# First attention: the first batch's first steps are held in front of the weights' on each engine, and the first weights load in three parts

## The chip, the cores and the metric

The kernel runs on one core of a Trainium2 chip. A core has five engines that run side by side, each through its own list of instructions in a fixed order: TensorE (PE, matrix products; PEld is its loading of weights), VectorE (DVE), ScalarE (ACT), GpSimd (POOL) and SyncE (SP, which here issues most of the transfers). An instruction waits until the results it reads are there, and everything behind it in its engine's list waits with it. The metric is the device time in microseconds (us) of one execution, lower is better; the median of several runs is what is compared.

## The reference, cut to what matters

Four layers work in turn on x of shape (4, 512, 128): each is a cross attention on a context of 32 rows and a feed-forward part. Only the beginning of the first layer is touched:

```python
x = x + L0_xattn(layernorm(x), ctx)       # the first attention
x = x + L0_ffn(layernorm(x))              # 8 experts, each token goes to one
...

def L0_xattn(tgt, memory, ...):
    qkv = tgt @ qkv_w.T + qkv_b
    q, k, v = jnp.split(qkv, 3, axis=-1)
    ...                                    # scores masked to their diagonal: attn is the identity
    sa = einsum('bnm,bmc->bnc', attn, v) @ sa_out_w.T + sa_out_b
    x = _ln(tgt + sa, ln1_g, ln1_b)
    ...                                    # cross attention of 8 heads with the context
    x = _ln(x + ca, ln2_g, ln2_b)
    ff = relu(x @ lin1_w.T + lin1_b) @ lin2_w.T + lin2_b
    return _ln(x + ff, ln3_g, ln3_b)
```

Because the self attention sees its diagonal alone, it is one product of the normalised x with a matrix that is made from `qkv_w` and `sa_out_w`.

## The kernel before

**Tiling.** A batch is 512 tokens, held as 4 tiles of 128 tokens by 128 columns. Everything is float32. A step of a batch is mostly one instruction over 128x512, or four over 128x128. A float32 product appears in the profile as two matmuls where it isn't a transposition, so "four products" is `x8`.

**Who sets the order.** The program is written as Python generators. `together` takes one step of each generator in turn, so the written order is a mixture of the chains; its argument `late` says in which round each chain enters. Out of that a scheduler makes the list of each engine when the program is built: it takes what it believes to be ready, by the written order where several are. So a change at one place can reorder the lists a long way on. `tc.issue_after(instruction)` puts all that is written inside its scope behind that instruction, on that instruction's engine. The object `queued` holds such scopes open until the tables of activation functions are next exchanged, in the second layer.

**The loads.** They are issued in the written order: batch 0's x (256 KB) on SP and the constants (`cst`) on ACT; then on SP the columns and rows of biases, the first weights `w0` (896 KB: sa_v, sa_o, ca_q, ca_k, ca_v, ca_o of 128 columns each, lin1 and lin2 of 512), x1; on ACT `adds`; then on SP x2, x3, `w1`, the first experts' weights and the masks. An issue on SP waits until an earlier transfer that used the same of eight semaphores has landed.

**The chains of the first attention.** `l0_weights` makes the folded weights: a matrix for the self attention (L477 to L484: `folded`, two products, a copy to `w_sa`), then kT of the context (`scaled_keys`, L295 and L297), the keys per batch (`folded_keys`: POOL L266, PE L319, ACT L321), the values (L338, L343), and a folded bias of lin1 (L506, L507). `attend0(g)` does one batch:

- a normalisation of x (`normed`): DVE statistics L203, L204, L206; ACT L208, L209; DVE L213 to L216, the shift c by L225 and L227; ACT L230 writes `xn`. POOL L516 adds a bias to x in place.
- `transposed`: PE L244, ACT L246; the self attention's product PE L256 and the sum y on DVE L468
- a second normalisation (DVE L232 writes z) and its transposition
- the cross attention in two halves (`attend`): PE L396, DVE L381 and L382, ACT L383, PE L409, ACT L411, PE L415, DVE L424 and L425; then the output product (L244, L246, L256) and a second y (L468)
- a normalisation with ACT's L230, the feed-forward part (PE L538, ACT L539, PE L544, a third y at L468), a last normalisation, and POOL's L558 and L559, which add the result to x (DVE for batch 3)

`noted(g)` follows in the same chain: it normalises the new x (L203 again, L234), writes it to memory, transposes it and makes the routing logits (PE L578, DVE L586). After all four batches the routing is completed, and POOL gathers tokens by it (L811).

The stage is started by these lines:

```python
    together(
        [
            l0_weights(w0),
            *(queue(attend0(g), noted(g)) for g in range(B)),
            early(),
            queue(ready("few1", l1_weights()), ready("slots", l1_ffn_weights()), ready("few2", l2_weights())),
        ],
        late={0: 0, 1: 0, 2: 3, 3: 6, 4: 9, 5: 14, 6: 14},
    )
```

Of the kernel before, what the change touches and what calls it, by code (L numbers as in the profile page):

```python
# [13 lines left out]
ALU = mybir.AluOpType  # L14
AX = mybir.AxisListType

P = 128
D = 128
B = 4
# [15 lines left out]
_W0 = [("sa_v", 128), ("sa_o", 128), ("ca_q", 128), ("ca_k", 128), ("ca_v", 128), ("ca_o", 128),  # L35
       ("lin1", 512), ("lin2", 512)]
# [18 lines left out]
def _offsets(spec):  # L55
    at, n = {}, 0
    for name, cols in spec:
        at[name] = (n, n + cols)
        n += cols
    return at, n  # L60
# [11 lines left out]
def tile_kernel(ctx: ExitStack, tc: tile.TileContext, I, out):  # L72
    nc = tc.nc
    const = ctx.enter_context(tc.tile_pool(name="const", bufs=1))
# [11 lines left out]
    l0 = l0_scope.enter_context(tc.tile_pool(name="l0", bufs=1))  # L86

    def psum(name="pt", fill=0):


        pt = ps.tile([P, 512], F32, tag="ps", name=name)
        for _ in range(fill):
            nc.tensor.matmul(pt[:, :P], lhsT=ident, rhs=ident, start=True, stop=True)  # L93
        return pt

    def small(cols, name="small", dtype=F32):
        return sm.tile([P, cols], dtype, tag=f"{name}{cols}", name=name)
# [2 lines left out]


    wide = {}

    def packed(key, spec, rows=P, pool=const, queue=nc.sync):
        at, n = _offsets(spec)
        t = pool.tile([rows, n], F32, tag=key, name=key)
        queue.dma_start(t, I[key])
        for name in ("switch", "router", "w_g"):
            if name in at:
                wide[name] = t[:, at[name][0] : at[name][0] + P]  # L110
        return {name: t[:, a:b] for name, (a, b) in at.items()}
# [9 lines left out]
    def together(chains, skew=0, late=()):  # L121


        waiting = [(late[i] if i in late else i * skew, c) for i, c in enumerate(chains)]
        running = []
        now = 0
        while waiting or running:
            running += [c for at, c in waiting if at == now]
            waiting = [(at, c) for at, c in waiting if at > now]
            for c in list(running):  # L130
                try:
                    next(c)
                except StopIteration:
                    running.remove(c)
            now += 1

    def queue(*steps):

        for c in steps:
            yield from c  # L140

    def batch(g):
        xg = const.tile([P, NJ, D], F32, tag=f"x{g}", name=f"x{g}")
        nc.sync.dma_start(xg, I["x"][g].rearrange("(j p) d -> p j d", p=P))
        return xg

    X = [batch(0)]
    C = packed("cst", _CST, queue=nc.scalar)
    col = packed("cols", _COLS)
    row = packed("rows", _ROWS, rows=1)  # L150
    W = packed("w0", _W0, pool=l0)
    X.append(batch(1))
    adds = const.tile([P, len(_ADDS), D], F32, tag="adds", name="adds")
    nc.scalar.dma_start(adds, I["adds"].partition_broadcast(P))
    add = {name: adds[:, i, :] for i, name in enumerate(_ADDS)}
    X += [batch(2), batch(3)]
    W.update(packed("w1", _W1))
    f0w1 = moe.tile([P, NEXP, 512], F32, tag="w1", name="f0w1")
    f0w2 = moe.tile([P, NEXP, 4, D], F32, tag="w2", name="f0w2")
# [11 lines left out]
    ident = C["ident"]  # L171
# [17 lines left out]
    queued = ctx.enter_context(ExitStack())  # L189
# [8 lines left out]
    def moments(src, p=P, n=NJ):  # L198

        st = sm.tile([P, n, 6], F32, tag=f"st{n}", name="st")  # L200
        mv = sm.tile([P, n, 2], F32, tag=f"mv{n}", name="mv")
        for j in range(n):
            nc.vector.bn_stats(st[:p, j, :], src[:, j, :])  # L203
            nc.vector.bn_aggr(mv[:p, j, :], st[:p, j, :])  # L204
        v = small(n, "v")[:p]
        nc.vector.tensor_scalar(v, mv[:p, :, 1], EPS, None, ALU.add)  # L206
        y = small(n, "y")[:p]
        nc.scalar.activation(y, v, AF.Ln)  # L208
        nc.scalar.activation(y, y, AF.Exp, scale=-0.5)  # L209
        yield  # L210

        t = small(n, "t")[:p]
        nc.vector.tensor_tensor(t, y, y, ALU.mult)  # L213
        nc.vector.scalar_tensor_tensor(t, t, -0.5, v, ALU.mult, ALU.mult)
        r = small(n, "r")[:p]
        nc.vector.scalar_tensor_tensor(r, t, 1.5, y, ALU.add, ALU.mult)  # L216
        return mv[:p], r

    def normed(src, tag, plus=0.0, act=False, p=P, n=NJ, bufs=B, pool=wk, into=None):

        mv, r = yield from moments(src, p, n)
        y = pool.tile([P, n, D], F32, tag=tag, name=tag, bufs=bufs) if into is None else into
        if plus or act:
            c = small(n, "c")[:p]
            nc.vector.scalar_tensor_tensor(c, mv[:, :, 0], -1.0, r, ALU.mult, ALU.mult)  # L225
            if plus:
                nc.vector.tensor_scalar(c, c, plus, None, ALU.add)  # L227
        for j in range(n):
            if act:
                nc.scalar.activation(y[:p, j, :], src[:, j, :], AF.Identity, bias=c[:, j : j + 1], scale=r[:, j : j + 1])  # L230
            elif plus:
                nc.vector.tensor_scalar(y[:p, j, :], src[:, j, :], r[:, j : j + 1], c[:, j : j + 1], ALU.mult, ALU.add)  # L232
            else:
                nc.vector.tensor_scalar(  # L234
                    y[:p, j, :], src[:, j, :], mv[:, j, 0:1], r[:, j : j + 1], ALU.subtract, ALU.mult
                )
        yield
        return y

    def transposed(src, tag="xnT", fill=0):  # L240

        pt = psum(fill=fill)
        for j in range(NJ):
            nc.tensor.transpose(pt[:, j * P : (j + 1) * P], src[:, j, :], ident)  # L244
        y = wk.tile([P, S], F32, tag=tag, name=tag, bufs=B)
        nc.scalar.copy(y, pt)  # L246
        yield
        return y

# [42 lines left out]
    def scaled_keys(w, bias, scale, rows=P):  # L292

        pt = psum()
        nc.tensor.matmul(pt[:rows, : B * M], lhsT=w, rhs=C["ctxT"], start=True, stop=True)  # L295
        kT = wk.tile([P, B * M], F32, tag="kTc", name="kTc")
        nc.vector.tensor_scalar(kT[:rows], pt[:rows, : B * M], 0.0 if bias is None else bias, scale, ALU.add, ALU.mult)  # L297
        return kT
# [175 lines left out]
    def l0_weights(w):  # L474


        fa = folded(W["sa_v"], bias=col["sa_bv"])  # L477
        ob = l0.tile([1, D], F32, tag="ob", name="ob")
        nc.vector.tensor_scalar(ob, row["sa_o_b"], 1.0 / D, None, ALU.mult)
        pt = psum()  # L480
        nc.tensor.matmul(pt[:, :D], lhsT=ones_row, rhs=ob, start=True, stop=False)
        nc.tensor.matmul(pt[:, :D], lhsT=fa, rhs=W["sa_o"], start=False, stop=True)
        w["sa"] = l0.tile([P, D], F32, tag="w_sa", name="w_sa")
        nc.scalar.copy(w["sa"], pt[:, :D])  # L484
        yield
        kT = scaled_keys(W["ca_k"], col["ca_bk"], 0.25)
        wq = folded(W["ca_q"], col["ca_bq"], add["ln1_g"], add["ln1_b"])
        with_value_bias("ca_o_b", col["ca_bv"], W["ca_o"])
        yield
        w["keys"] = padded(l0, "keys0", 8 * M)  # L490
        for b in range(B):
            folded_keys(w["keys"], wq, kT, 8, C["hm8"], bs=(b,))
            if b % 2:
                yield
        w["vals"] = head_values("v0", context_rep, W["ca_v"], 8, M, C["vm8"], C["hi32"], l0)


        w["rest"] = rest = l0.tile([P, 2, D], F32, tag="rest", name="rest")
        nc.gpsimd.tensor_tensor(rest[:, 0], add["ln1_b"], add["ln1_g"], ALU.subtract)
        nc.gpsimd.tensor_tensor(rest[:, 0], rest[:, 0], add["ca_o_b"], ALU.add)  # L500
        nc.gpsimd.tensor_tensor(rest[:, 1], add["ln2_b"], add["lin2_b"], ALU.add)
        yield
        w["lin1_b"] = lin1_b = l0.tile([P, 4], F32, tag="lin1b", name="lin1_b")
        pt = psum()
        for f in range(4):
            nc.tensor.matmul(pt[:, f : f + 1], lhsT=W["lin1"][:, f * P : (f + 1) * P], rhs=col["ln2_b"], start=True, stop=True)  # L506
        nc.vector.tensor_tensor(lin1_b, pt[:, :4], col["lin1_b"], ALU.add)  # L507
        nc.gpsimd.tensor_scalar(W["lin1"], W["lin1"], col["ln2_g"], None, ALU.mult)
        yield
# [833 lines left out]
    w0 = {}  # L1343
    attend0 = l0_xattn(w0)
# [17 lines left out]
    def noted(g):  # L1362
        yield from route0(g)
        routed0.append(g)

    def early():

        while len(routed0) < B - 1:
            yield
        yield from part0(0, (B - 1) * NJ)  # L1370

    together(
        [
            l0_weights(w0),
            *(queue(attend0(g), noted(g)) for g in range(B)),
            early(),
            queue(ready("few1", l1_weights()), ready("slots", l1_ffn_weights()), ready("few2", l2_weights())),
        ],
# [285 lines left out]
```

## Time and profile before

| | us |
|---|---|
| median of 3 runs | 649.58 |
| lowest and highest run | 647.67 and 649.80 |
| the profiled execution | 642.63 |
| its span | 640.8 |
| gather of routed tokens starts, in the span | 146.16 |
| TensorE busy | 530.2 |
| VectorE busy | 331.7 |
| ScalarE busy | 237.9 |
| GpSimd busy | 150.6 |

The profile is of one execution and can differ from the median. In a timeline a line is: start in us from the span's start, duration in us, engine, line of the program, operation, what it writes and reads with shapes, how many instructions are merged (`x4`), and in brackets how long the engine had been idle and what ended the wait. Instructions of one group can be interleaved with others, so groups overlap. A table of stretches gives, for each, the busy time of the engines named, with the number of instructions; then the clock granted to TensorE (1.00 is full), the share of the transfer engines and GB/s.

### The profile page before, as it was taken

To read this page: it belongs to the slowest core of one execution; us is meant where nothing else is said; L and a number is where in the kernel's file an instruction comes from. 1 tells how busy PE (TensorE), PEld (TensorE's weight loads), DVE (VectorE), ACT (ScalarE), POOL (GpSimd) and SP (SyncE) were. 2 spreads that over 40 slices of the span, in tenths; PEclk is the share of its full clock that TensorE was granted. 3 is DMA by queue.
4 is the path that set the end of the run, shared out by engine and by line. 5 is a ranking of instruction groups with operands and counts; after the bars stand their busy time and mean duration, and the time that the engine had idled before them with its cause. 6 is when DMAs were issued, how large, how long until landed. Compare 5 with 4: busy or idle time off the path is not lost.

```text
span 640.8 us, 9381 instructions
## 1 busy us (share of the span) xinstructions
PE 530.2 (83%) x3344; PEld 417.3 (65%) x3344; DVE 331.7 (52%) x1379; ACT 237.9 (37%) x538; POOL 150.6 (24%) x187
## 2 busy tenths in 40 slices
PE   2568889836998888899644999991899799999996
PEld 2557667626986664799431788881478676767764
DVE  4686654583397542688762222214777763323232
ACT  2353555411245621443210234341655343343432
POOL 4243233306503001100477155442200000000000
PEclk9977998966997999999657899997699999999999
DMA  8970001131296008300011321015300000000000
GB/s 321 313 226 18 18 17 50 34 115 38 84 360 243 1 1 277 126 2 2 29 52 51 114 80 62 30 35 151 131 1 2 1 2 1 17 1 16 17 2 16
DMA packets 42000, 48.94 MB, mean 76 GB/s; under 512 B 5129, under 2 KB 29074, under 8 KB 41762
## 3 DMA queue, kind: packets, MB, share of 16 engines
q1 hardware_dynamic: 38706, 40.64, 19.2%
q0 software_dynamic: 2816, 5.82, 2.8%
q10 hardware_dynamic: 432, 1.89, 0.8%
q8 instruction: 26, 0.43, 0.3%
q14 instruction: 20, 0.16, 0.1%
HBM read 37.81 MB, written 13.22 MB: 80 GB/s over the span
## 4 chain that ended last, share of the span: by engine, by line
PE 44%; POOL 10%; issue 8%; DVE 8%; ACT 4%; DMA 3%; SPq 0%; POOLq 0%; DVEq 0%; ACTq 0%
PE pt L1325 9%; PE pt L1277 9%; POOL yd L1214 6%; PE pt L93 3%; PE pt L244 3%; PE po L415 3%; PE pt L396 3%; PE pt L578 2%; PE pt L256 2%; PE pt L1060 2%; DMA yg<-yd 1%; PE pt L409 1%; POOL xs L689 1%; PE pt L996 1%; PE pt L463 1%
## 5 line engine op out<-in xcount | busy, mean ns | idle before, releaser
L1325 PEld LDWEIGHTS pt<-f3w,hT 128*128 128x128 f32 x512 | 65.4, 191 | 33.2 <-ACT hT L1278 19.3
L1335 DVE SCALAR_TENSOR_TENSOR x<-pt,gates,x 128x128 f32<-128x128 f32 x128 | 36.0, 345 | 76.9 <-PE pt L1325 76.8
L1278 ACT ACTIVATE hT<-pt,cols 128x512 f32<-128x512 f32 x64 | 44.0, 687 | 73.5 <-PE pt L1277 73.0
L1325 PE MATMUL pt<-f3w,hT 128*128 128x128 f32 x512 | 68.5, 277 | 1.0 <-ACT hT L1278 0.6
L1277 PE MATMUL pt<-xnT,f3w 128*128 128x512 f32 x128 | 65.1, 597 | 0.0
L1214 POOL DMA_INDIRECT yd<-ye,to x40 | 38.3, 958 | 47.4 <-DVE ye L1210 25.4
L689 POOL DMA_INDIRECT xs<-rows,to x32 | 31.3, 978 | 61.3 <-issue 58.3
L1198 ACT ACTIVATE hT<-pt 128x384 f32<-128x384 f32 (+1 forms) x64 | 27.6, 438 | 45.0 <-PE pt L1195 43.6
L203 DVE BATCH_NORM_STATS2 st<-x 128x6 f32<-128x128 f32 x128 | 32.5, 273 | 19.2 <-POOL x L559 13.2
L1203 PEld LDWEIGHTS pt<-f2w,hT 128*128 128x128 f32 x320 | 39.6, 191 | 3.7 <-ACT hT L1198 0.7
L246 ACT COPY xnT<-pt 128x512 f32<-128x512 f32 x40 | 23.4, 584 | 49.0 <-PE pt L244 48.9
L1203 PE MATMUL pt<-f2w,hT 128*128 128x128 f32 x320 | 40.7, 279 | 0.0
L93 PE MATMUL pt<-cst 128*128 128x128 f32 x292 | 40.0, 281 | 0.0
L93 PEld LDWEIGHTS pt<-cst 128*128 128x128 f32 x292 | 36.9, 196 | 2.2 <-issue 1.5
L1195 PE MATMUL pt<-exT,f2w 128*128 128x256 f32 (+1 forms) x128 | 37.4, 434 | 0.4 <-DVE exT L845 0.4
L244 PE MATMUL pt<-cst,xn 128*128 128x128 f32 x80 | 19.3, 334 | 20.2 <-ACT xn L230 16.5
L1210 DVE TENSOR_TENSOR ye<-pt,gate 128x384 f32<-128x384 f32 (+1 forms) x16 | 7.9, 491 | 51.5 <-PE pt L1203 51.5
L244 PEld LDWEIGHTS pt<-cst,xn 128*128 128x128 f32 x80 | 12.2, 161 | 28.3 <-ACT xn L230 20.5
L381 DVE TENSOR_REDUCE mx<-pt 128x16 f32<-128x512 f32 (+1 forms) x32 | 22.0, 688 | 14.0 <-PE pt L396 13.5
L415 PEld LDWEIGHTS po<-v,aT 128*128 128x128 f32 x192 | 25.3, 203 | 5.1 <-issue 3.2
L1195 PEld LDWEIGHTS pt<-exT,f2w 128*128 128x128 f32 x128 | 23.0, 190 | 8.2 <-DVE exT L845 0.7
L396 PE MATMUL pt<-keys,xnT 128*128 128x256 f32 (+1 forms) x64 | 27.5, 538 | 0.9 <-ACT xnT L246 0.9
(340 smaller groups left out, 1072.7 us busy)
## 6 DMA issues: line engine op xcount, KB each, us to landing
e_wg<-in_e_wg SPq DMA_DIRECT2D x8, 512.0 KB, 6.9
e_w<-in_e_w SPq DMA_DIRECT2D x8, 512.0 KB, 8.9
yg<-yd SPq DMA_DIRECT2D x12, 256.0 KB, 4.3
xs<-in_empty SPq DMA_DIRECT2D x1, 2620.0 KB, 11.6
xg<-xs SPq DMA_DIRECT2D x8, 327.5 KB, 3.1
f0w<-in_f_w SPq DMA_DIRECT2D x1, 2048.0 KB, 13.2
yd<-zero SPq DMA_DIRECT2D x8, 256.0 KB, 3.5
ew<-in_e_w SPq DMA_DIRECT2D x8, 256.0 KB, 4.9
```

The costliest lines, as they stand in the source:

```text
L93: nc.tensor.matmul(pt[:, :P], lhsT=ident, rhs=ident, start=True, stop=True)
L244: nc.tensor.transpose(pt[:, j * P : (j + 1) * P], src[:, j, :], ident)
L396: nc.tensor.matmul(pt[:, j * nk : (j + 1) * nk], lhsT=xT[:, (j0 + j) * P : (j0 + j + 1) * P], rhs=keys, start=True, stop=True,)
L415: nc.tensor.matmul(po[:, k, :], lhsT=aT[:, k * P : (k + 1) * P], rhs=of(values[k % nch], cols + hpc, g), start=True, stop=True,)
L689: ins = nc.gpsimd.indirect_dma_start(out=xs[:], out_offset=bass.IndirectOffsetOnAxis(ap=to[:, k, j : j + 1], axis=0), in_=rows[g][:, j, :] ...
L1195: nc.tensor.matmul(pt[:, : m * P], lhsT=f2w1[:, e, f * P : (f + 1) * P], rhs=xT, start=True, stop=True)
L1203: nc.tensor.matmul(pt[:, c * D : (c + 1) * D], lhsT=hT[:, f, c * P : (c + 1) * P], rhs=f2w2[:, e, f, :], start=f == 0, stop=f == 3,)
L1214: ins = nc.gpsimd.indirect_dma_start(out=yd[:], out_offset=bass.IndirectOffsetOnAxis(ap=to[:, c0 + c : c0 + c + 1], axis=0), in_=y[:, c, : ...
L1277: nc.tensor.matmul(pt, lhsT=f3w1[:, e, f * P : (f + 1) * P], rhs=xnT[g], start=True, stop=True)
L1278: nc.scalar.activation(hT[:, f, :], pt, AF.Gelu, bias=col["f3_b1"][:, 2 * e + f : 2 * e + f + 1])
L1325: nc.tensor.matmul(pt[:, j, :], lhsT=hT[:, f, j * P : (j + 1) * P], rhs=f3w2[:, e, f, :], start=f == 0, stop=f == 1,)
L1335: nc.vector.scalar_tensor_tensor(xj, pt[:, j, :], ge, xj, ALU.mult, ALU.add)
```

## The change

Three things are done. First, `w0` is loaded by three transfers into the same tile: columns 0 to 256 (sa_v, sa_o) and 256 to 768 (the four `ca` matrices) where the one load was, and columns 768 on (lin1, lin2) behind x3. Second, the first four steps of batch 0 (`attend0(0)`) are taken by hand ahead of the chains' mixture, with the first step of `l0_weights` between the second and the third. Third, `issue_after` holds all that is written from then on behind three instructions of batch 0: on VectorE behind its last shift (L227), from the first weights on; on TensorE behind its last transposition (L244) and on ScalarE behind the copy of the transposed tile (L246), from the fourth step on. The other chains enter in the same rounds as before.

```diff
-    def packed(key, spec, rows=P, pool=const, queue=nc.sync):
+    later, lasts = [], {}
+
+    def packed(key, spec, rows=P, pool=const, queue=nc.sync, load=True):
         at, n = _offsets(spec)
         t = pool.tile([rows, n], F32, tag=key, name=key)
-        queue.dma_start(t, I[key])
+        if load:
+            queue.dma_start(t, I[key])
+        else:
+            later.append(t)
...
-    W = packed("w0", _W0, pool=l0)
+
+    W = packed("w0", _W0, pool=l0, load=False)
+    for a, b in ((0, 256), (256, 768)):
+        nc.sync.dma_start(later[0][:, a:b], I["w0"][:, a:b])
     X.append(batch(1))
...
     X += [batch(2), batch(3)]
+    nc.sync.dma_start(later[0][:, 768:], I["w0"][:, 768:])
     W.update(packed("w1", _W1))
...
-                nc.vector.tensor_scalar(c, c, plus, None, ALU.add)
+                lasts["shift"] = nc.vector.tensor_scalar(c, c, plus, None, ALU.add).ins
...
-            nc.tensor.transpose(pt[:, j * P : (j + 1) * P], src[:, j, :], ident)
+            lasts["turned"] = nc.tensor.transpose(pt[:, j * P : (j + 1) * P], src[:, j, :], ident).ins
...
-        nc.scalar.copy(y, pt)
+        lasts["copied"] = nc.scalar.copy(y, pt).ins
...
+    ahead, weights = queue(attend0(0), noted(0)), l0_weights(w0)
+    next(ahead)
+    next(ahead)
+    queued.enter_context(tc.issue_after(lasts["shift"]))
+    next(weights)
+    next(ahead)
+    queued.enter_context(tc.issue_after(lasts["turned"]))
+    queued.enter_context(tc.issue_after(lasts["copied"]))
+    next(ahead)
     together(
         [
-            l0_weights(w0),
-            *(queue(attend0(g), noted(g)) for g in range(B)),
+            weights,
+            ahead,
+            *(queue(attend0(g), noted(g)) for g in range(1, B)),
             early(),
```

In the built program the number of instructions on each of the four computing engines is the same; SP issues two transfers more. The lists of all engines stand in another order up to the gather at L811. Lines in the text are those of the kernel before.

## The prediction

> **What bounds the kernel now.** I read the time first, then the busy time by stretch, then the timeline of the first 146 us, and the chain of waits last. The profiled execution took 642.63 us (a span of 640.8 us and 1.8 us around it); the median shown is 649.58 us, 1.1% more. My sum gives a difference to the span, and I add that difference to the median. In the chain of waits the first piece is the gather of routed tokens at 146.16 us (POOL, L811), which needs the routing of all four batches. So the first attention counts through one moment only: when the last batch (3) is through its attention, feed-forward and routing. From there on the program is the same.
>
> ```profile
> 0.00:50.00 50.00, 26.54 (x117) 22.07 (x118) 32.92 (x162) 18.28 (x47) 19.06 (x37) 0.90 0.82 276
> 50.00:130.00 80.00, 69.28 (x416) 55.54 (x415) 45.72 (x212) 40.42 (x102) 25.94 (x28) 0.94 0.11 32
> 130.00:146.00 16.00, 5.21 (x37) 3.80 (x35) 12.88 (x59) 1.71 (x7) 0.52 (x4) 0.56 0.29 92
> ```
>
> Busy time of PE, PEld, DVE, ACT and POOL, then the granted clock: PE is busy 26.5 of the first 50 us, 69.3 of the next 80, 5.2 of the last 16. The middle is nearly PE's own; the end is a chain of short DVE steps of batch 3. The timeline shows the start:
>
> ```profile
> 10.14 0.29 DVE L279 TENSOR_REDUCE off<-w 128x1 f32<-128x128 f32 x1 [1.58 <-DMA w<-in_w]
> 12.41 0.40 DVE L227 TENSOR_SCALAR c<-c 128x4 f32<-128x4 f32 x1
> 12.85 1.65 ACT L230 ACTIVATE xn<-x,c,r 128x128 f32<-128x128 f32 x4 [0.16 <-DVE c L227]
> 22.99 1.92 PE L256 MATMUL pt<-w_sa,xnT 128*128 128x128 f32 x8
> 24.95 0.69 DVE L468 TENSOR_TENSOR y<-pt,xn 128x512 f32<-128x512 f32 x1 [1.42 <-PE pt L256]
> 30.02 1.12 DVE L232 TENSOR_SCALAR z<-y,r,c 128x128 f32<-128x128 f32 x4
> ```
>
> Batch 0's L225 and L227 stand behind DVE work on the weights that waits until 10.14 us for the 896 KB load. Its first sum y (L468) comes at 24.95 us, its second normalisation (L232) at 30.02.
>
> **The change, part by part.** *The load in three.* 128 KB and 256 KB go ahead of x1, x2, x3, and 512 KB behind them. The whole landed at 10.1 us, batch 0's x at 5.8. At the same rate the first 128 KB land by about 7 us (estimate: x at 5.8 plus 1/7 of 4.3 us, and a small load in front), before DVE wants them. The rest is wanted by L506 (26.2 us before) and stands behind transfers of the same total. SP gets two more issues, at 0.4 us each (0.36 for the old one). What is queued behind on SP are the expert weights, the masks, the zeroing of yd and xs; each comes 1 to 1.5 us later, because one expert load now waits for the `adds` load (9.5 us) where it was issued at 8.2. Their cover is long: f0w is first read after 149 us, and the masks at 35.8 us without a wait. Cost 0; if the masks were late, L381 of batch 0 behind them, up to 1.5 us.
>
> *Batch 0 in front.* DVE is through L216 at 8.56 us and no longer waits, and L479 (0.3) is behind too: L227 ends at about 8.7, ACT's L230 at 10.4 (12.85 + 1.65 = 14.5 before). On PE one weight product (L482) still stands between the four transposes. It needs L289, and that needs L479, L287, L283 (`adds`, 9.5 us), L288, L284: 10.6. L482 0.8, three transposes 0.8, the copy 0.6 and L256 1.9 + 0.1 give y at 15.0 us. Here the POOL gets in:
>
> ```profile
> 14.58 1.26 POOL L516 TENSOR_TENSOR x<-x,adds 128x512 f32<-128x512 f32 x1 [1.79 <-ACT xn L230]
> 14.84 1.03 DVE L206 TENSOR_SCALAR v<-mv 128x4 f32<-128x4 f32 x1
> 19.24 1.26 POOL L516 TENSOR_TENSOR x<-x,adds 128x512 f32<-128x512 f32 x1 [2.58 <-ACT xn L230]
> 19.31 1.21 DVE L287 TENSOR_TENSOR off<-off,cols 128x1 f32<-128x1 f32 x1
> ```
>
> A DVE step of 0.16 us that begins inside L516 ends when L516 ends. The moved L516 starts at 10.4 us, right where L288 and L289 stand, so L289 ends late by 0 to 1.3 us. I take 1.0: y at 16.0 us, 9 us earlier. The Trainium skill (SBUF — State Buffer, Who interferes with whom) has a rule for this: a DVE `tensor_scalar` or a two-input op and a GpSimd op exclude each other on a shared port for the whole instruction, the first to issue winning. The rows agree; by the rule alone the loss could also fall on L516, and the sum would be 1.0 lower.
>
> From y the second normalisation took 5.1 us (24.95 to 30.02). In the new order ACT's L209 for it stands behind the third copy of the keys (L321), whose POOL product (0.66) now starts after y. That adds about 2 us: z at 24 us, 6 earlier.
>
> *What is put behind.* Batch 1's L230 (17.5 us before) now follows batch 0's second transposes (26 us), and on ACT batch 0's attention copy (L411) waits behind one piece of batch 2's L230. Adding up queue by queue with the rows' durations, batch 1's y moves from 33.29 to about 35, batch 3's y from 51.03 to about 53.5: 2.5 us late, while batch 0's second y comes at 51 where it came at 63.30. PE has then done more work than before: one L409 (0.6), one L415 (1.06), L244 (0.6) and L256 (1.06) of batch 0, together 3.3 us. So at 53.5 us PE stands where it stood at 51.0 + 3.3 = 54.3. Before the L409 that was at 62.99, PE has moreover done L538 of batch 0 (3.6) and its L244 (0.6), 4.2 us: I get 66 against 67. One microsecond ahead, used up by waits of 0.8 us each for L371 and L383: at the last L396 of batch 3 (ended 81.26, plus the 3.74 of L544 now done before it: 85.0) the two are even.
>
> *Where it is lost.* From there to the end of batch 1's L544:
>
> ```profile
> 81.31 3.74 PE L544 MATMUL pt<-w,hT 128*128 128x128 f32 x32
> 93.72 1.26 POOL L559 TENSOR_TENSOR x<-x,z 128x512 f32<-128x512 f32 x1
> 95.01 0.49 DVE L203 BATCH_NORM_STATS2 st<-x 128x6 f32<-128x128 f32 x2 [4.30 <-POOL x L559]
> 95.94 1.03 PE L371 MATMUL pt<-w,vTc 64*32 64x128 f32 x8 [2.28 <-DVE vTc L365]
> 96.90 5.47 PE L544 MATMUL pt<-w,hT 128*128 128x128 f32 x32
> ```
>
> DVE reads batch 0's new x (L203) and stands 4.30 us for POOL; behind it L365, so PE stands 2.28 us and then runs L544 at half clock (5.47 for 3.74). In the changed order that same L203 comes earlier: between L381 and L382 of batch 3's last softmax, and before L214 and L225 of batch 1's next normalisation, whose L230 on ACT also stands behind that softmax's exp. PE's L244 of batch 1, which waited for nothing at 85.78, now has no work before it. Batch 0's new x: its L468 at 75, the normalisation 7, POOL 2 x 1.27 in a row, 86. Then four L203 with L204 (1.2), L382 (0.7), L225 and small steps (0.7), exp (0.63), L230 (0.5): 89.5 us, and PE wants it at 86. I take 3.6 us of idle PE. After an idle stretch the clock falls: PE idle from 27.7 to 30.4 us, then a granted clock of 0.50 until 36. So 2.3 us of work behind the gap takes 1.5 longer. The Trainium skill (TensorE: Matmul & The Clock Gate, Part 1) puts the gate's window at about 3.4 us; by it a gap of 3.6 may or may not be enough (1.5 or 0), but the row shows 2.7 us doing it.
>
> Before, this stretch took 102.37 − 81.26 = 21.1 us, of which L544 of batch 0 (3.7) is gone: 17.4. Added: L244 and L578 of batch 0's routing (0.6 + 1.06), idle 3.6, half clock 1.5. Gone: the wait for L365 (2.28) and L544's half clock (1.73). Sum 20.1: **2.7 us later**. The tail is batch 1 and 3 as before, without the two routing products: −0.3. So +2.4 us: span 643.2, and on the median **652.0 us**. The unknown wait, bounded: 0 (DVE gets there late anyway) to 5.3 us (3.6 + 1.65: PE stands until all four pieces of batch 1's L230 are done).
>
> **Rivals.**
> *The head start carries through (faster).* PE is busy 87% from 50 to 130 us, which speaks for it; that batch 3 starts 2.5 us late speaks against. If the new idle and half clock stay away, the stretch takes 20.1 − 5.1 = 15.0 for 17.4; with the 1 us ahead and the tail: 2.4 + 1.0 + 0.3 = 3.7 us faster, 645.9.
> *Nothing arrives.* Batch 3 ends the stage and the change moves batch 0; L482 among the transposes keeps part of the head start even there. Wait gained and wait made cancel: 649.6.
> *Half clock through the middle (slower still).* In the first 55 us the new order leaves PE idle in two gaps of some 3 to 4 us (before batch 1's L244 at 40 us, and for batch 3's L230 at 46 to 49). If the clock stays at 0.50 over the 6 us of work after them, that is 3 us more; it decides from one gap above 2.7 us on. With the sum: +5.4, 655.0.
>
> **How the numbers follow.** A measurement here tells 0.3% (1.95 us) from no change. Forecast 0.38, with its own range 650.5 to 654.5 (0.04 of it within 0.3%); slower still 0.18; nothing 0.14; head start 0.30. Slower 0.34 + 0.18 = 0.52, same 0.18, faster 0.30. The range takes in the head start at its own uncertainty (645) and the wait's upper bound with the half clock (2.4 + 1.7 + 3 = 7.1): 645 to 657.
>
> **What would show it.** Batch 0's L468 near 16 us and L232 near 24; batch 3's first L468 at 53 to 54; an idle PE of 3 us and more before batch 1's L244 near 86 us, released by ACT's L230; L544 of batch 1 in 3.7 us and not 5.5; the gather at 148 to 149 us and not 146.2; after it, the same distances. If the gather comes before 144 us, the accounting by PE's work was wrong and the start did carry through; if the gather moves but the total does not, I misread what follows it.

## The result, and the profile after

The changed kernel takes 654.51 us (median of 21 runs, 647.27 to 658.01) where the kernel before took 648.33 beside it (21 runs, 646.57 to 652.84). The ratio is 1.0068, 95% interval 1.0047 to 1.0089: about 4.4 us slower. It leaves out the three longest runs of the changed kernel, which lie over 1.5% above its fastest; with them the medians are 6.2 us apart. Forecast were 652.0 us and a loss of 2.4 us. The profiled execution took 651.58 us (span 649.8). Lines are now those of the changed kernel: from L203 on, 8 higher than before (L244 is L252).

Busy time by stretch (us, PE, PEld, DVE, ACT, POOL, then PE's granted clock, share of the transfer engines, GB/s), changed kernel:

```profile
0.00:50.00 50.00, 28.93 (x137) 24.11 (x137) 32.63 (x166) 18.86 (x49) 18.92 (x37) 0.83 0.85 281
50.00:130.00 80.00, 66.75 (x385) 51.55 (x383) 43.23 (x195) 39.93 (x100) 25.99 (x29) 0.91 0.08 24
130.00:149.00 19.00, 7.21 (x47) 5.31 (x47) 15.80 (x73) 2.30 (x8) 0.52 (x4) 0.62 0.33 97
```

PE runs 137 matmuls in the first 50 us, where it was 117, so the head start is real (the 2.4 us more of busy time are in part the lower clock, 0.83 for 0.90). But in the next 80 us it does less (385 matmuls for 416, 66.75 us for 69.28) although part of that time runs at a lower clock (0.91 for 0.94), and the end comes later. The start, from the timeline of the changed kernel:

```profile
10.26 0.80 PE L490 MATMUL pt<-w,fa 128*128 128x128 f32 x2
...
10.53 1.27 POOL L524 TENSOR_TENSOR x<-x,adds 128x512 f32<-128x512 f32 x1 [1.78 <-ACT xn L238]
...
10.77 1.05 DVE L293 TENSOR_TENSOR off<-off,so 128x1 f32<-128x1 f32 x1
...
14.55 0.69 DVE L476 TENSOR_TENSOR y<-pt,xn 128x512 f32<-128x512 f32 x1 [2.03 <-PE pt L264]
...
21.19 1.09 DVE L240 TENSOR_SCALAR z<-y,r,c 128x128 f32<-128x128 f32 x4
```

Batch 0's first y comes at 14.55 us instead of 24.95, its z at 21.19 instead of 30.02. L293, a step of 0.16 us, takes 1.05 and ends with POOL's L524: the collision that the prediction expected, but at another step and off the path to y. The weight product that y needs (L490) had begun before L524 did; L293 belongs to another fold, which ends in the keys per batch (L327). The late wait, same timeline:

```profile
84.08 1.03 PE L404 MATMUL pt<-keys,xnT 128*128 128x256 f32 x4
...
84.60 1.27 POOL L566 TENSOR_TENSOR z<-z,adds 128x512 f32<-128x512 f32 x1 [3.94 <-ACT z L238]
...
85.05 0.84 DVE L221 TENSOR_TENSOR t<-y 128x4 f32<-128x4 f32 x1
...
85.81 0.68 DVE L389 TENSOR_REDUCE mx<-pt 128x16 f32<-128x512 f32 x1
...
85.95 1.26 POOL L567 TENSOR_TENSOR x<-x,z 128x512 f32<-128x512 f32 x1
...
87.25 0.49 DVE L211 BATCH_NORM_STATS2 st<-x 128x6 f32<-128x128 f32 x2 [0.56 <-POOL x L567]
...
88.39 0.66 DVE L390 TENSOR_TENSOR att<-pt,mx 128x512 f32<-128x512 f32 x1
...
90.24 0.46 PE L252 MATMUL pt<-cst,z 128*128 128x128 f32 x1 [4.11 <-ACT z L238]
```

Batch 3's last scores (L404) end at 85.11. Between its softmax's two DVE steps (L389, L390) stand four statistics of batch 0's new x, which wait for POOL; batch 1's shift is behind them too, and PE idles 4.11 us until ACT's L238 has made batch 1's z. The gather, which ends the stage, comes 2.97 us later than the 146.16 of before:

```profile
149.13 1.18 POOL L819 DMA_INDIRECT xg<-xd,inv  x1 [11.42 <-DVE to L813]
```

From there to the end it is 500.7 us, where it was 494.7. Some 5.3 of these other 6 us arise between 311 and 370 us, in the routing of the second layer, where DVE is slow (first fence: changed kernel; second: kernel before, where the lines are 8 lower):

```profile
327.72 0.18 DVE L647 TENSOR_TENSOR at<-at,b_rev 128x32 bf16<-128x32 bf16 x1
328.43 0.19 DVE L648 TENSOR_REDUCE w<-at 128x4 f32<-128x32 bf16 x1 [0.54 <-DVE at L647]
329.13 0.19 DVE L650 TENSOR_TENSOR ohs<-at,w 128x32 bf16<-128x32 bf16 x1 [0.51 <-issue]
```

```profile
322.60 0.20 DVE L639 TENSOR_TENSOR at<-at,b_rev 128x32 bf16<-128x32 bf16 x1
322.84 0.19 DVE L640 TENSOR_REDUCE w<-at 128x4 f32<-128x32 bf16 x1
```

The steps themselves take 0.19 us in both; but one follows another after 0.70 us instead of 0.22. The experiments had to say whether that belongs to the change.

### The profile page after: what moved, and what is told of

It reads as the page before. It is cut to its first block, busy times and chain, and to the rows that moved or that the text cites. A ratio compares the mean times of both kernels' runs of the same rounds, so it can differ in the third digit from the quotient of the medians.

```text
span 649.8 us, 9386 instructions
## 1 busy us (share of the span) xinstructions
PE 529.3 (81%) x3344; PEld 414.5 (64%) x3344; DVE 332.8 (51%) x1379; ACT 238.8 (37%) x538; POOL 151.1 (23%) x187
## 4 chain that ended last, share of the span: by engine, by line
PE 41%; POOL 11%; issue 9%; DVE 8%; ACT 4%; DMA 3%; another core or an unknown queue 1%; SPq 0%; POOLq 0%; DVEq 0%; ACTq 0%
PE pt L1333 9%; PE pt L1285 9%; POOL yd L1222 6%; PE pt L93 3%; PE po L423 3%; PE pt L252 3%; PE pt L404 2%; POOL xs L697 2%; PE pt L264 2%; PE pt L1068 2%; PE pt L417 1%; DMA yg<-yd 1%; DVE st L211 1%; POOL yd L829 1%; PE pt L586 1%
## 5 line engine op out<-in xcount | busy, mean ns | idle before, releaser
L697 POOL DMA_INDIRECT xs<-rows,to x32 | 31.6, 988 | 66.3 <-issue 65.7
L211 DVE BATCH_NORM_STATS2 st<-x 128x6 f32<-128x128 f32 x128 | 32.3, 272 | 14.4 <-POOL x L567 8.6
L252 PE MATMUL pt<-cst,xn 128*128 128x128 f32 x80 | 20.1, 335 | 23.9 <-ACT xn L238 19.8
L252 PEld LDWEIGHTS pt<-cst,xn 128*128 128x128 f32 x80 | 12.2, 161 | 32.0 <-ACT xn L238 23.9
L417 PE MATMUL pt<-cst,att 128*128 128x128 f32 x128 | 22.6, 295 | 8.7 <-ACT att L391 8.5
L389 DVE TENSOR_REDUCE mx<-pt 128x16 f32<-128x512 f32 (+1 forms) x32 | 21.9, 684 | 13.9 <-PE pt L404 13.6
L404 PE MATMUL pt<-keys,xnT 128*128 128x256 f32 (+1 forms) x64 | 27.7, 541 | 0.9 <-ACT xnT L254 0.9
```

The costliest lines, as they stand in the source:

```text
L252: lasts["turned"] = nc.tensor.transpose(pt[:, j * P : (j + 1) * P], src[:, j, :], ident).ins
L404: nc.tensor.matmul(pt[:, j * nk : (j + 1) * nk], lhsT=xT[:, (j0 + j) * P : (j0 + j + 1) * P], rhs=keys, start=True, stop=True,)
L697: ins = nc.gpsimd.indirect_dma_start(out=xs[:], out_offset=bass.IndirectOffsetOnAxis(ap=to[:, k, j : j + 1], axis=0), in_=rows[g][:, j, :] ...
```

## The experiments

Theory A: the first attention loses by the late wait near 86 us and PE's half clock behind it, as predicted. Theory B: PE's half clock in the middle (57 to 66 us) loses as well. Rivals: the load or the holds themselves cost; DVE and ACT set the pace and PE's idle time is a symptom; the slow DVE stretch is the change's own. Ratios are to the kernel before, run beside on the same chip; the intervals are 95%. "Gather" and "gather to end" are of one profile each. L404 "comes" where it starts, unless its end is named.

| run | what | ratio | interval | gather, us | gather to end, us |
|---|---|---|---|---|---|
| e1 | changed kernel again | 1.0065 | 1.0032 to 1.0098 | 147.17 | 496.0 |
| e2 | load in three alone | 1.0017 | 0.9992 to 1.0042 | 145.75 | 494.5 |
| e3 | order alone, one load | 1.0160 | 1.0125 to 1.0195 | 153.34 | 494.4 |
| e4 | routing of batch 0 later | 1.0017 | 0.9993 to 1.0041 | 146.48 | 493.4 |
| e5 | e4, last additions on DVE | 1.0012 | 0.9988 to 1.0037 | 147.27 | 502.5 |
| e6 | 2 fillings of 3.5 us | 1.0116 | 1.0077 to 1.0154 | 152.81 | 502.8 |
| e7 | e5 and e6, one filling more | 1.0078 | 1.0047 to 1.0109 | 149.22 | 500.9 |
| e8 | 2 fillings of 1.75 us | 1.0015 | 0.9987 to 1.0042 | 145.73 | 497.7 |
| e9 | e5 and e8, one filling more | 0.9995 | 0.9967 to 1.0023 | 141.01 | 496.4 |
| e10 | kernel before again | | | 143.67 | 498.2 |
| e11 | no holds | 1.0077 | 1.0049 to 1.0104 | 149.79 | 495.9 |
| e12 | e9, two fillings more | 1.0005 | 0.9977 to 1.0032 | 143.51 | 494.9 |

**e1: the changed kernel once more.** No edit.

> The changed kernel once more, nothing altered. Theory: the first attention costs what its first profile showed, and the rest of that profile's 9.0 us did not belong to the change. So the gather (L819) is again at 149.1 us within 0.5 (146.16 before), batch 1's transposition L252 again waits about 4.1 us for ACT's z near 90 us, and PE's half clock again lies at 57 to 67 us; but the stretch from 323 to 337 us, in which DVE took 0.7 us per small step instead of 0.22, is not there, and the span is 644 to 645 us instead of 649.8. Rival: the slow stretch belongs to the changed program; then it is there again near 323 us and the span is 649 to 650.

Median 645.39 us (before: 642.64). The slow DVE stretch isn't there; the wait before batch 1's L252 is again 4.11 us. The gather came 2 us earlier than expected (147.17 for 149.1), with the half clock in the middle at 47.2 to 50.6 and 57.5 to 64.3 us instead of 56.2 to 66.4. The ratio is the same as in the first comparison without the slow stretch, so that stretch is not what makes the change slower (if the kernel before had it on that chip too; see e10).

**e2 and e3: the two halves of the change.** e2 keeps the three loads and starts the chains as before; e3 keeps the start and has one load:

```diff
-    W = packed("w0", _W0, pool=l0, load=False)
-    for a, b in ((0, 256), (256, 768)):
-        nc.sync.dma_start(later[0][:, a:b], I["w0"][:, a:b])
+    W = packed("w0", _W0, pool=l0)
...
-    nc.sync.dma_start(later[0][:, 768:], I["w0"][:, 768:])
```

> The load of w0 in three parts alone; the chains start as in the kernel before. Theory: the load in three costs nothing by itself; it may reorder some of DVE's first steps, because the planner believes the first columns to be there sooner. Batch 0's first y (L476) between 24 and 27 us, gather at 146 to 147.5 us, ratio to the kernel before 0.998 to 1.003. Rival: the two more issues and the later lin1 and lin2 cost in themselves; gather at 148 us or later, ratio 1.004 or more.

> Batch 0's steps held in front as in the changed kernel, but w0 in one load as before. Theory: the order does it, not the load. Batch 0's first y 15 to 17 us (14.55 with the three loads, 24.95 before), a wait of 3 us or more for ACT's z of batch 1 near 90 us, gather at 148.5 to 150 us, ratio to the kernel before 1.003 to 1.008. Rival: the load in three is needed for the loss; gather at 146 to 147 us, ratio 0.998 to 1.002.

The load alone changes nothing that can be measured (first y 25.63 us, gather 145.75). The order alone is far worse than expected: 1.6% slower. Batch 0's first y is at 16.92 us, 2.4 us behind e1, because DVE waits for the whole load until 10.27 us; by batch 3's last L404 (L401 in e3; 88.46 for 82.28) that has become 6.2 us, and it stays so to the gather. The two halves don't add up: the early columns are worth nothing alone, and 0.95% (1.0160 − 1.0065, from runs of one chip) once batch 0 stands in front. How 2.4 us become 6.2 was not taken apart; the lists of PE, DVE and ACT also stand in a somewhat different order in e3, and from 20 to 72 us its profile has 20.5 us of half clock for 17.1.

**e4: the late wait moved.** The diff:

```diff
-    ahead, weights = queue(attend0(0), noted(0)), l0_weights(w0)
+    ahead, weights = queue(attend0(0), iter([None] * 3), noted(0)), l0_weights(w0)
```

> The changed kernel, with batch 0's routing entering the mixture three rounds later; nothing else. On DVE the statistics of batch 0's new x (L211), which wait for POOL's L567, now stand behind batch 1's shift L233 and batch 1's second y, no longer between the two steps of batch 3's last softmax. Theory: that wait is what cost the middle. L390 of batch 3 comes near 86.5 us instead of 88.39, batch 1's z (L238) near 87 instead of 89.71, PE's wait before batch 1's L252 is under 1.5 us instead of 4.11, no half clock follows it, and the gather comes at 144.5 to 146 us instead of 149.1: 3 to 4.5 us less than the changed kernel, ratio to the kernel before 0.996 to 1.002. Rival: batch 3's and batch 1's own chains decide, and the wait only fills a pause that is there anyway; gather at 148 to 149.5 us, ratio as the changed kernel's.

The wait before batch 1's L252 falls from 4.11 to 2.80 us, less than expected; the ratio falls to 1.0017, as expected. The intervals of e1 and e4 overlap; the difference of the two ratios is 0.48%, 3.1 us. In the two profiles, which have the same half-clock times up to 88 us, the gather gains only 0.7 us (146.48, where 144.5 to 146 was expected). Half clock did follow the wait, against the expectation, and lasted 6.8 us instead of 3.4: batch 1's L546 took 5.30 us for 3.60. What is left of the wait is seen in the timeline of e4:

```profile
82.85 1.27 POOL L566 TENSOR_TENSOR z<-z,adds 128x512 f32<-128x512 f32 x1 [3.94 <-ACT z L238]
...
83.30 0.84 DVE L221 TENSOR_TENSOR t<-y 128x4 f32<-128x4 f32 x1
...
84.20 1.26 POOL L567 TENSOR_TENSOR x<-x,z 128x512 f32<-128x512 f32 x1
...
84.86 0.62 DVE L222 SCALAR_TENSOR_TENSOR t<-t,v 128x4 f32<-128x4 f32 x1
...
85.40 0.68 DVE L390 TENSOR_TENSOR att<-pt,mx 128x512 f32<-128x512 f32 x1
```

Two DVE steps of 0.16 us end where POOL's two steps end (84.12 and 85.46), without reading what these write. So POOL still holds DVE up, 1.1 us in front of L390.

**e5: the additions on DVE.** On top of e4, with the three rounds placed ahead of the additions:

```diff
+            for _ in range(3 if g == 0 else 0):
+                yield
-            engine = nc.vector if last else nc.gpsimd
+            engine = nc.vector if last or g == 0 else nc.gpsimd
```

> The changed kernel with batch 0's routing three rounds later, and with batch 0's two last additions (L566, L567) on DVE instead of POOL. In the run with the routing later alone, two small DVE steps that begin while POOL is in these additions (L221 at 83.30 us, L222 at 84.86) took 0.84 and 0.62 us for 0.16 each: 1.1 us in front of L390 of batch 3. Theory: that goes, two additions of 0.69 us come to DVE, the first of them in front of L389, so about 0.4 to 1.1 us is left: PE's wait before batch 1's L252 is 1.7 to 2.5 us (2.80 with the routing later alone), batch 1's z (L238) at 85.5 to 86.3 us, ratio to the kernel before 0.997 to 1.001. Rival: the two additions cost DVE as much as they free; wait 2.8 us or more, ratio 1.001 to 1.004.

The wait is 2.20 us, inside what was expected. The ratio 1.0012 is just outside the theory's range and inside the rival's, and can't be told from e4's. Batch 1's z came at 90.70 us, not at 85.5 to 86.3: this profile is 2.5 us behind e1's from batch 1's y on and has half clock from 59.0 to 69.3.

**e6 and e8: the two idle times in the middle filled.** PE gets products of the identity, which are overwritten, in front of two transpositions; `n` is 16 in e6 and 8 in e8:

```diff
-            tT = yield from transposed(tgt)
+            tT = yield from transposed(tgt, fill=n if g == B - 1 else 0)
...
-            zT = yield from transposed(z)
+            zT = yield from transposed(z, fill=n if g == 0 else 0)
```

> The changed kernel with 16 products of the identity (0.11 us each at full clock, their result is overwritten) on PE in front of batch 3's first transposition and 16 in front of batch 0's transposition after its second y: in the two idle times of 2.2 to 2.9 us at 46 and 56 us. Theory: the half clock that follows these two costs time in the changed kernel. The clock stays at 1.00 from 46 to 66 us, where it was 0.50 for 10.2 us in both profiles of the changed kernel; batch 3's last L404 comes 2 to 4 us earlier than the 82.28 of the second profile, the wait before batch 1's L252 near 88 us is still there, and the ratio to the kernel before is 0.998 to 1.003 (1.0065 without the filling). Rival: the chains of DVE and ACT set the pace there, and PE at half clock keeps up with them; L404 within 1 us of 82.3, ratio 1.005 to 1.008.

> The two fillings at half their size. In the run before, one product of the identity was two matmuls, so 16 of them took 3.5 to 3.7 us and not 1.8, more than the idle time of 2.2 to 2.9 us that they were to fill; the kernel got slower although the clock stayed at 1.00 from 46 to 66 us. With 8 each (1.75 us) they end before the work behind them is ready. Theory: the half clock in the middle costs time; it stays away (1.00 from 46 to 62 us at least), batch 0's L546 starts 2 us or more before the 60.1 to 61.6 of the changed kernel's profiles, ratio to the kernel before 0.999 to 1.004. Rival: DVE and ACT set the pace in the middle and PE at full clock only waits longer; L546 at 60 to 62 us, ratio 1.005 to 1.008 as the changed kernel's.

e6 is a miss by arithmetic: a product is two matmuls of 0.11 us, so a filling took 3.5 to 3.7 us for idle times of 2.2 to 2.9. The clock stayed at 1.00 from 45.9 to 66.3 us as expected, but the last L404 came at 88.02, and the kernel got slower than the changed one. e8 has the right size. The first profile of the changed kernel and that of e8 happen to have the half clock at the same times up to 42.5 us, and the first y of each batch agrees within 0.12 us (batch 3's 51.42 and 51.30). Batch 0's second y comes 0.66 us earlier in e8 (48.59): with the filling in its list, PE took batch 0's output product (L264) first. PE's busy time and clock from there, first the changed kernel, then e8:

```profile
52.00:56.00 4.00, 1.93 (x10) 1.00 0.01 2
56.00:60.00 4.00, 3.13 (x15) 0.52 0.00 0
60.00:64.00 4.00, 3.74 (x10) 0.50 0.00 0
64.00:68.00 4.00, 4.00 (x12) 0.70 0.00 0
```

```profile
52.00:56.00 4.00, 3.62 (x26) 1.00 0.01 2
56.00:60.00 4.00, 2.58 (x16) 1.00 0.00 0
60.00:64.00 4.00, 4.00 (x13) 1.00 0.02 4
64.00:68.00 4.00, 2.87 (x21) 1.00 0.00 0
```

In the first stretch the changed kernel is busy 1.93 of 4 us, and the clock is at half until 66.4; with the filling it stays at 1.00. Batch 0's L546 starts 1.0 us earlier only (60.62 for 61.61; the theory wanted 2 us or more, and 60.62 is inside the rival's range) but takes 3.60 us for 5.98, and batch 3's last L404 comes at 80.71 instead of 84.08: 3.4 us, of which up to 0.7 can be the changed order. Against e1 (82.28) it is 1.6 us. The ratio falls from 1.0065 or 1.0068 (on other chips) to 1.0015, the theory's range; the difference of 0.5% is itself uncertain by 0.4%. So the half clock of the middle costs the changed kernel time, as theory B says. It isn't the changed kernel's alone, though: between 46 and 72 us PE has 10.2 us of it in each of the five profiles with the new start, three loads and no filling (the first, e1, e4, e5, e11), 6.8 and 0 in the two of the kernel before, and 3.4 in e2.

**e7, e9 and e12: all of it together, for a version faster than both.** e9 has the routing later, the additions on DVE, the fillings of 8 and one of 5 in front of batch 1's L252; e7 the same with 16, 16 and 8; e12 is e9 with two fillings more, at 28 and 39 us.

> All of it together: routing of batch 0 three rounds later, its last additions on DVE, the two fillings, and 8 products of the identity more in front of batch 1's transposition L252 near 87 us. Theory: the two losses are apart from each other and their ends add up; gather at 141 to 144 us, ratio to the kernel before 0.990 to 0.997, which would be faster than both kernels. Rival: what is won in front is used up by waiting for batch 3's softmax, as the head start was; gather at 145 to 147 us, ratio 0.998 to 1.003.

> Batch 0's routing three rounds later, its last additions on DVE, and fillings of 8, 8 and 5 products of the identity (1.75, 1.75 and 1.1 us) in front of batch 3's first transposition, batch 0's second and batch 1's second one. Theory: no half clock from 46 us to the end of batch 1's L552, gather at 142 to 145 us, ratio to the kernel before 0.993 to 0.999. Rival: the chains of DVE and ACT set the pace; gather at 146 to 148 us, ratio 1.000 to 1.003, as without the fillings (1.0012).

> The version with the routing later, the additions on DVE and the three fillings, with two fillings more: 3 and 5 products of the identity (0.7 and 1.1 us at full clock, twice that at half) on PE in front of the transpositions L417 of batch 0 and batch 1 near 28 and 39 us, where PE is idle 1.6 and 2.6 us and where the clock is 0.50 for 10 us of 28.9 to 42.6. Theory: PE sets the pace there as it does from 46 us on; some 2 to 4 us are won, gather at 137 to 140 us if the other windows fall as in the run before, ratio to the kernel before 0.992 to 0.998. Rival: before 46 us DVE, ACT and the late weights set the pace, nothing is won or the fillings get in the way; ratio 0.999 to 1.004.

e7 (expected 0.990 to 0.997, measured 1.0078) pays for its long fillings as e6 does. The timeline of e9 has no wait and a full clock where the changed kernel idled; the filling (1.3 us) and two products (L264, L417) now stand in front of L252 (lines behind L565 are 2 higher here):

```profile
83.33 0.68 DVE L390 TENSOR_TENSOR att<-pt,mx 128x512 f32<-128x512 f32 x1
...
84.00 0.68 DVE L569 TENSOR_TENSOR x<-x,z 128x512 f32<-128x512 f32 x1
...
84.57 1.63 ACT L238 ACTIVATE z<-y,c,r 128x128 f32<-128x128 f32 x4
...
85.21 0.27 PE L252 MATMUL pt<-cst,z 128*128 128x128 f32 x1
```

e8 and e9 have the half clock at the same times and the same marks up to L404 (80.71 in both), so this pair of profiles prices the late wait with what follows it, and the three edits of e9 together: the gather comes at 141.01 for 145.73, 4.7 us. The runs show less: the ratios of e8 and e9 differ by 0.20% (1.3 us), those of e6 and e7 by 0.38% (2.5 us), those of e1 and e4 by 0.48%, each with an uncertainty of 0.4 to 0.5%. Against the two profiles of the kernel before (146.16 and 143.67) e9's gather is 2.7 to 5.2 us earlier. But over twelve runs e9 scatters from 638.4 to 647.2 us and its ratio, 0.9995, misses the expected 0.993 to 0.999 and can't be told from 1. That the two losses add up isn't shown either: below e1's ratio e4 and e5 lie by 0.48 and 0.53%, e8 by 0.50%, and e9, which has both remedies, by 0.70%. e12 came out in its rival's range (1.0005, gather 143.51 for the expected 137 to 140). In its profile the same filling did not keep the clock up: behind three short waits and the beginning of one of 2.08 us (57.2 to 59.3) came half clock, from 57.7 to 64.5 us. A version that is faster than the kernel before has not been shown.

**e10: the kernel before once more.**

> The kernel before once more, for a profile of it beside the others of this call. The two chips so far differ: the kernel before took 642.6 us on one and 649.0 on the other, and all three profiles from the second have a stretch of some 14 us after 321 us in which a small step of DVE takes 0.7 us for 0.22, as the first profile of the changed kernel has; none from the first chip has it. Theory: the stretch belongs to the chip and is in the kernel before too, where the chip is one of the second kind: DVE's slow stretch near 319 to 333 us, span 645 to 649, and the distance from the gather to the end about 500 us instead of 494.7. On a chip of the first kind no profile of this call has it. Rival: it belongs to the changed order; then this profile has none while the other two have it.

This ran on a third chip, with the kernel before at 642.57 us, and none of the three profiles from it (e8, e9, e10) has the slow stretch. So the expectation was met in its weaker half only. What speaks for the chip: the stretch is in all three profiles from one chip, also in e5 to e7, whose lists differ; in none of the nine from three others, the changed kernel itself among them (e1); and the kernel before itself takes 6 us longer where it was seen (648.3 and 649.0 us for 642.6, 642.6 and 643.1). No profile of the kernel before from such a chip was taken, so that it has the stretch there too is inferred.

The profile also gives the marks of the kernel before at full clock: it has none at half from 44.3 to 95.5 us, as e8 has none from 42.5 to 86.9. First e10, then e8 (L409 and L396 are the changed kernel's L417 and L404):

```profile
60.78 0.60 PE L409 MATMUL pt<-cst,att 128*128 128x128 f32 x4
...
77.80 1.03 PE L396 MATMUL pt<-keys,xnT 128*128 128x256 f32 x4
```

```profile
64.06 0.60 PE L417 MATMUL pt<-cst,att 128*128 128x128 f32 x4
```

**e11: no holds.** The three `issue_after` left out; steps and loads as in the changed kernel.

> The changed kernel without its three holds: batch 0's four steps are still taken by hand in front of the mixture and w0 still loads in three. (In the built program the holds on PE and ACT move nothing; without the one on DVE, batch 0's shift L235 stands six places later, between small steps on the weights; w_sa's copy L492 and three of four transpositions change places.) Theory: the hand-taken steps make the order, and the holds decide 2 us at most at the start: batch 0's first y at 14.5 to 17 us, the wait of some 4 us before batch 1's L252 near 88 us is there, gather at 147 to 150 us, ratio to the kernel before 1.004 to 1.010. Rival: the hold on DVE carries the change; without it batch 0's y falls back behind 20 us and the ratio to 0.998 to 1.002.

Ratio 1.0077: as the changed kernel. Batch 0's first y is at 17.37 us (just above the expected 14.5 to 17, short of the rival's 20), the wait is 4.11. In the built program the holds on PE and ACT change nothing; the one on DVE is worth some 3 us at the start and nothing measurable at the end. The four steps taken by hand make the order.

## Why the prediction was right, and where not

The direction, the place and the mechanism of the late wait were right; the size was too small: +2.4 us forecast, +4.4 measured (3.0 to 5.8 by the interval).

- *The load in three, cost 0.* Right alone (e2). That it is needed for the rest, worth 0.95% there, was in the sum only as the early landing.
- *Batch 0 in front.* y 16.0 forecast, 14.55; z 24, 21.19: the head start is some 3 us larger at z than worked out. The 1.0 us for POOL's L524 came as 1.05 − 0.16 = 0.9, but on L293, which y does not wait for; so the 15.0 us without it was the better sum. Nor does every step that begins inside L516 end with it, as the prediction read the rows: in the kernel before, L204 began inside it at 14.63 us and took 0.18.
- *What is put behind.* Batch 1's y 35, measured 34.89; batch 3's y 53.5, measured 51.42; batch 0's second y 51, measured 49.25. The later batches lose less than forecast.
- *One microsecond ahead at 66, even at 85.0.* The second number was met (85.11, the end of batch 3's last L404), but in part by luck, since the profiles compared don't have the same clock in the middle. At full clock on both sides (e10 and e8) the marks come as worked out: with the same 4.2 us added, the kernel before stands at 60.78 + 4.2 = 65.0 us where e8 stands at 64.06, 0.9 us ahead; at the end of the last scores it is 78.83 + 3.74 = 82.57 against 81.74, still 0.8 ahead. The changed kernel as it is reached the mark of 66 at 67.43 and in e1 at 65.62, and against e8's 80.71 its half clock took 3.4 and 1.6 us by L404. That is the third rival's mechanism; it was priced at 3 us and given 0.18, beside the forecast and not in it, and its gaps were put at 40 and 46 to 49 us. In the first profile the one that counted is at 53.9 to 56.9. The sum held there because the profile that it starts from had lost 2.4 us to half clock as well (81.26 for e10's 78.83).
- *Where it is lost: idle 3.6, half clock 1.5.* Measured 4.11 idle, and half clock from 90.3 to 93.7 us. From the end of batch 3's L404 to the end of batch 1's L552, 20.1 us were forecast and 21.2 came (85.11 to 106.31), 6.2 more than the 15.0 without losses, for 5.1 forecast. At the gather it is 4.7 us from e8 to e9, and in the runs 1.3 to 3.1 (above). At full clock in the middle on both sides the gather comes 2.1 us later than before (145.73 in e8, 143.67 in e10), near the forecast 2.4. Without either loss the head start does carry through in the profile (e9: 2.7 to 5.2 us at the gather), about the 3.7 us of the first rival, but not in the runs (0.9995); the second rival, that nothing arrives, is excluded by the interval of the ratio. L552 of batch 1 took 3.74 us, not 5.47, as forecast; a wait before L379 of 0.47 us was left of 2.28. That L211 waits for POOL is the smaller part (0.56 us): its place in DVE's list, between L389 and L390, and POOL's L566 holding L221 do the rest, as e4 and e5 show by undoing one after the other (4.11, 2.80, 2.20).
- *The tail, −0.3.* Measured −1.0 (42.82 us from the end of L552 to the gather, 43.79 before).
- *The same distances after the gather.* 493.4 to 498.2 us in ten profiles with the kernel before at 494.7 and 498.2; the 500.7 of the first profile is the slow stretch, which by the two comparisons is not the change's (as inferred under e10).

The term that was mis-sized is then the middle: the sum took the half clock there as a rival instead of a term. Measured from e8, the changed kernel's two profiles lose 2.4 us by it at the gather in the mean (149.13 and 147.17 for 145.73); measured from e10, the kernel before loses 1.2 in the mean of its own two (146.16 and 143.67). So 1.2 us are the change's, beside the 2.1 above, as far as two profiles of each tell. The four pairs put the loss at the gather between 1.0 and 5.5 us, 3.2 in the mean; the rest up to 4.4 is within the interval and was not looked for.

## What to carry to other kernels

Work moved ahead on one engine arrives somewhere else later: look up which instruction of the favoured chain waits for another engine, and what stands behind it in its own list, above all steps of chains that were on time. Where PE has idle times of 2 to 3 us, or several short ones close together, count the clock after them as a term of the sum, in the kernel before as well as in the changed one, and weigh a short filling; one that is longer than the idle time costs more than the clock (e6). A profile of one execution can differ from another of the same kernel by 2 us at one mark through the clock alone, so compare pairs whose clock falls at the same times.

## What the runs showed of the hardware

PE's clock changes on a grid: every stretch of one granted clock in these traces, but for the last one of each, is a multiple of 3.41 us (3.4, 6.8, 10.2, 13.7 and so on), and the grid lies elsewhere from run to run (the half clock of the middle begins at 56.2 and 57.5 us in two profiles of the changed kernel). So the idle time at one place of the program was followed by 10.2 us of half clock in one of them and by 6.8 in the other. The Trainium skill (TensorE: Matmul & The Clock Gate, Part 1) describes such a free-running window; the runs agree with its length. Its advice (Why this matters for your kernels) to avoid idle times above about 3 us is too wide for this case: an idle time of 2.17 us (53.6 to 55.8 us in e1) was followed by 6.8 us at half clock. What the traces show in front of each fall is a window of the grid in which PE did little. In the 14 profiles 145 windows at full clock were followed by half clock, and PE was busy at most 0.65 of each; none of the 1823 windows in which it was busy more was followed by half clock, of 153 with 0.41 to 0.65 half were, and all 68 with less were. In the kernel before, PE was busy 1.84 of 3.42 us from 56.72 to 60.14, with no idle time above 1.45, and then had half clock; in the changed kernel 1.19 us from 52.74 to 56.16; in e8, with the filling, 2.88 there, and the clock stayed.

POOL's products and sums of two tiles (TENSOR_TENSOR over 128x512, 1.27 us) hold some of DVE's steps and not others. In the 14 profiles every one of 55 steps t<-y (128x4, 0.16 us) that began inside one, more than 0.35 us before its end, ended with it; of 402 steps of the batch statistics (BATCH_NORM_STATS2 and BATCH_NORM_AGGREGATE) none did.

DVE can be slow in one place of a program: in four of the 14 profiles (the first of the changed kernel, and the three from e5's chip) there are steps of 0.19 us 0.70 us apart instead of 0.22, and single stalls of 1.7 to 3.25 us, for some 14 us, each time in the second layer's routing. The cause isn't known.
